# Turning new queries and keys for attention: 32x32 blocks on VectorE in place of 128x128 transposes on TensorE

## The chip, the cores and the metric

The kernel runs on one core of one Trainium2 chip. A core has five engines with a queue of instructions each, worked through in order: TensorE (PE in the profile; its weight loads are PEld), VectorE (DVE), ScalarE (ACT), GpSimd (POOL) and SyncE (SP). They share an on-chip memory of 128 partitions (SBUF); TensorE writes into accumulators (PSUM, eight banks of 128 partitions by 512 fp32). Transfers are issued by SyncE and GpSimd and carried out by 16 DMA engines. The metric is the device time of one execution in microseconds, the median of several runs.

## The reference

A tensor `x` of 32 batches, 32 positions and 512 features passes four residual stages, all in fp32. Each stage chooses weights by a token of the batch. The change concerns the fourth, attention over a paged cache with new queries, keys and values:

```
q = einsum('bsd,ed->bse', x, Wq)   # 32 heads of 128
k = einsum('bsd,ed->bse', x, Wk)   #  8 heads of 128
v = einsum('bsd,ed->bse', x, Wv)   #  8 heads of 128
q = rope(rmsnorm(q, q_norm_w), pos);  k = rope(rmsnorm(k, k_norm_w), pos)
k_all = concat([k_cache[block_table], k]);  v_all = concat([v_cache[block_table], v])
x = x + softmax(mask(q @ k_all.T * SCALE)) @ v_all @ Wo.T
```

`rmsnorm` divides each head of a row by the root of the mean of its squares and multiplies by a weight of 128 numbers. `rope` turns pairs of features (a feature of the first half of the head with its partner in the second) by an angle that grows with the position.

## The kernel before

The 1,024 rows of `x` (batch and position) make 8 row tiles of 128, four batches each. The program has three parts that follow each other.

**Residual stages 0 to 2.** A loop written out by hand sets TensorE's order. Eight row tiles pass through a pipeline with an offset of one tile from step to step: a mixing matmul (`mix`), transposes of `x` (`x1t`, `x2t`, `x3t`, each four 128x128 transposes on TensorE into PSUM and one copy on ScalarE, L383 and L384), a low-rank product, the base product and the adapter product (`adapt`, L439). After each product VectorE adds the result to `xs`. In the last steps of the same loop the projection of chunk 0 is done for each row tile.

**Projections.** The weights of queries, keys and values are 12 chunks `c` of 512 columns: 0 to 7 queries, 8 and 9 keys, 10 and 11 values, each four heads of 128. For every chunk and row tile (`project`, 96 in all, 80 with queries or keys), TensorE adds up four matmuls in a PSUM bank (L263; the trace shows two records for each fp32 matmul). Then, for queries and keys:

- ScalarE squares the bank (`sq`, L279), VectorE sums per head (`ss`, L281), ScalarE takes the root (`rms`, L283), VectorE its reciprocal (`rinv`, L285).
- VectorE multiplies the bank by the cosine table times the weight (`ra`, L287) and, in two halves, by the sine table (`rs`, L291 and L297). GpSimd adds the two (L303).
- VectorE multiplies the sum by `rinv`, spread over each head (L304).
- `store_heads`, called two tiles later (one tile later in chunk 0): TensorE turns the four heads (L312), ScalarE copies the four turned blocks out of PSUM into `st` (L314), in the order batch, head, position, and SyncE stores `st` to DRAM (L322), into `q_d` or `k_d`, which hold, for each batch, 128 features by heads and positions.

Value tiles are copied by ScalarE into one of two buffers `vs` (L273) and stored (L274). Outside the two loops marked as written out by hand, a scheduler orders each engine's instructions when the program is built, by the order of the source and by what is ready. Buffers: five PSUM banks for projections (`a_mm`), two for transposes (`a_tr`), one for the low-rank product (`a_lo`); three buffers each of `ra`, `st` and the small columns, two of `sq` and `rs`; two of a chunk's weights `wq` (L257).

SyncE's queue holds, in one order, the loads of weights, the stores of L322 and L274, and the loads for attention. Pages of batch 0 are loaded while chunks 0 to 2 are projected (L149, keys by SyncE, values by GpSimd). When the last key tile has been stored, the projection's buffers are given up (`turn.close()`), and batch 1's home takes their place: its new keys and queries are read back from `k_d` and `q_d` (L199, L200) and its 16 pages of keys and of values are loaded. The new values of the first batches are read from `v_d` (L229) once value tiles are stored.

**Attention.** 32 batches of 8 key heads, 256 units, in an order written out by hand for all engines: scores (L590, L591), mask and row maximum on VectorE (L597), exponentials on ScalarE (L604), division, four transposes (L621), products with values (L641), and the output projection after every four batches (L677). Batch b+1's data are loaded while batch b is worked on.

The core of the tail that the change rewrites:

```
for h in range(REP):
    nc.tensor.transpose(pt[:, h, :], a[:, h, :], ident)
st = tp.tile([P, BT, REP * S], F32, tag="st", name=f"st_{c}_{t}")
nc.scalar.copy(
    st.rearrange("d b (h s) -> d h b s", h=REP),
    pt.rearrange("d h (b s) -> d h b s", b=BT),
)
```

Of the kernel before, what the change touches and what calls it, by code (L numbers as in the profile page):

```python
# [11 lines left out]
F32 = mybir.dt.float32  # L12
I32 = mybir.dt.int32
AF = mybir.ActivationFunctionType
ALU = mybir.AluOpType
AX = mybir.AxisListType
PSUM = bass.MemoryType.PSUM
DRAM = bass.MemoryType.DRAM

P = 128  # L20
B, S, HID = 32, 32, 512
D, HQ, HK = 128, 32, 8
REP = HQ // HK
PAGES, PSIZE, NPP = 64, 32, 16
L = NPP * PSIZE
LT = L + S
NT = B * S // P
BT = P // S
# [25 lines left out]
def cond_resid_kernel(  # L54
# [18 lines left out]
    nc = tc.nc  # L73
# [3 lines left out]
    dram = ctx.enter_context(tc.tile_pool(name="scratch", bufs=1, space=DRAM))  # L77


    q_d = dram.tile([B, D, HQ * S], F32, name="q_d")  # L80
    k_d = dram.tile([B, D, HK * S], F32, name="k_d")
    v_d = dram.tile([B * S, HK * D], F32, name="v_d")


# [18 lines left out]
    ident = const.tile([P, P], F32, name="ident")  # L103
# [78 lines left out]
    homes, kts, vts, vns, news = {}, {}, {}, {}, {}  # L182
# [4 lines left out]
    def load_keys(b: int):  # L187
# [7 lines left out]
            mask, key_f, len_f[:, b : b + 1], -1.0e30, ALU.is_ge, ALU.mult  # L195
        )

    def load_new_keys(b: int):
        nc.sync.dma_start(out=kts[b][:, NPP, :], in_=k_d[b])  # L199
        nc.sync.dma_start(out=news[b][0], in_=q_d[b])  # L200

    def page_keys(b: int):
        return [kts[b][:, n, :] for n in range(NPP)]
# [30 lines left out]
    with ExitStack() as pa:  # L234
# [2 lines left out]
        turn = pa.enter_context(ExitStack())  # L237
        wp = turn.enter_context(tc.tile_pool(name="a_w", bufs=1))
        tp = turn.enter_context(tc.tile_pool(name="a_t", bufs=3))
        ps_mm = pa.enter_context(tc.tile_pool(name="a_mm", bufs=5, space=PSUM))  # L240
        ps_tr = pa.enter_context(tc.tile_pool(name="a_tr", bufs=2, space=PSUM))
        ps_lo = pa.enter_context(tc.tile_pool(name="a_lo", bufs=1, space=PSUM))


        x3t = xp.tile([P, KC, NT * P], F32, name="x3t")
# [9 lines left out]
        def load_qkv(c: int):  # L255
            ws[c] = wqp.tile([P, KC, HID], F32, tag="wq", name=f"wq_{c}")
            nc.sync.dma_start(out=ws[c], in_=w_qkv[c])  # L257

        def project(c: int, t: int):
            w = ws[c]  # L260
            ps = ps_mm.tile([P, HID], F32, tag="mm", name=f"qkv_{c}_{t}")
            for k in range(KC):
                nc.tensor.matmul(  # L263
                    ps,
                    x3t[:, k, t * P : (t + 1) * P],
                    w[:, k, :],
                    start=(k == 0),
                    stop=(k == KC - 1),
                )
            if c >= (HQ + HK) // REP:  # L270
                c0 = (c - (HQ + HK) // REP) * HID
                vs = xp.tile([P, HID], F32, tag="vs", name=f"vs_{c}_{t}", bufs=2)
                nc.scalar.copy(vs, ps)  # L273
                nc.sync.dma_start(out=v_d[t * P : (t + 1) * P, c0 : c0 + HID], in_=vs)  # L274
                return None
            i = 0 if c < HQ // REP else 1
            ps4 = ps.rearrange("p (h d) -> p h d", h=REP)
            sq = tp.tile([P, REP, D], F32, tag="sq", name=f"sq_{c}_{t}", bufs=2)
            nc.scalar.activation(sq, ps4, AF.Square)  # L279
            ss = tp.tile([P, REP], F32, tag="ss", name=f"ss_{c}_{t}")  # L280
            nc.vector.tensor_reduce(ss, sq, AX.X, ALU.add)  # L281
            rms = tp.tile([P, REP], F32, tag="rms", name=f"rms_{c}_{t}")
            nc.scalar.activation(rms, ss, AF.Sqrt, bias=eps_t, scale=1.0 / D)  # L283
            rinv = tp.tile([P, REP], F32, tag="rinv", name=f"rinv_{c}_{t}")
            nc.vector.reciprocal(rinv, rms)  # L285
            a = tp.tile([P, REP, D], F32, tag="ra", name=f"ra_{c}_{t}")
            nc.vector.tensor_tensor(  # L287
                a, ps4, cw[:, i, t, :].unsqueeze(1).to_broadcast([P, REP, D]), ALU.mult
            )
            s = tp.tile([P, REP, D], F32, tag="rs", name=f"rs_{c}_{t}", bufs=2)  # L290
            nc.vector.tensor_tensor(  # L291
                s[:, :, :H2],
                ps4[:, :, H2:],
                sw[:, i, t, :H2].unsqueeze(1).to_broadcast([P, REP, H2]),
                ALU.mult,
            )
            nc.vector.tensor_tensor(  # L297
                s[:, :, H2:],
                ps4[:, :, :H2],
                sw[:, i, t, H2:].unsqueeze(1).to_broadcast([P, REP, H2]),  # L300
                ALU.mult,
            )
            nc.gpsimd.tensor_tensor(a, a, s, ALU.add)  # L303
            nc.vector.tensor_tensor(  # L304
                a, a, rinv.unsqueeze(2).to_broadcast([P, REP, D]), ALU.mult
            )
            return c, t, a

        def store_heads(c: int, t: int, a):
            pt = ps_tr.tile([P, REP, P], F32, tag="tr", name=f"qt_ps_{c}_{t}")  # L310
            for h in range(REP):
                nc.tensor.transpose(pt[:, h, :], a[:, h, :], ident)  # L312
            st = tp.tile([P, BT, REP * S], F32, tag="st", name=f"st_{c}_{t}")
            nc.scalar.copy(  # L314
                st.rearrange("d b (h s) -> d h b s", h=REP),
                pt.rearrange("d h (b s) -> d h b s", b=BT),
            )
            if c < HQ // REP:
                dst, c0 = q_d, c * REP * S
            else:  # L320
                dst, c0 = k_d, (c - HQ // REP) * REP * S
            nc.sync.dma_start(  # L322
                out=dst[t * BT : (t + 1) * BT, :, c0 : c0 + REP * S].rearrange(
                    "b d x -> d b x"
                ),
                in_=st,
            )

        ready = []
# [1 line left out]
        def projected(c: int, t: int, lag: int):  # L331
            done = project(c, t)
            if done is not None:
                ready.append(done)
            if len(ready) > lag or (done is None and ready):
                store_heads(*ready.pop(0))

        with ExitStack() as p1:
# [169 lines left out]
            with tc.manual_schedule(engines={mybir.EngineType.PE}):  # L508
# [4 lines left out]
                for n in range(NT + 5):  # L513
# [24 lines left out]
                    if n == 4:  # L538
                        with tc.issue_after(picked_keys[-1]):
                            load_qkv(1)  # L540

        wop = ctx.enter_context(tc.tile_pool(name="b_wo", bufs=1, side="right"))
        wo = wop.tile([P, HQ, HID], F32, name="wo")
        vnp = ctx.enter_context(tc.tile_pool(name="b_vn", bufs=3, side="right"))
# [2 lines left out]
        for c in range(1, NCH):  # L547
            if c + 1 < NCH:
                load_qkv(c + 1)
            if c == 2:  # L550
                load_pages(0)
                load_values(0)
            if 3 <= c < 7:
                hs = slice((c - 3) * HQ // 4, (c - 2) * HQ // 4)
                nc.sync.dma_start(out=wo[:, hs, :], in_=w_o[:, hs, :])
            if c == (HQ + HK) // REP:

                while ready:
                    store_heads(*ready.pop(0))
                turn.close()  # L560
                load_new_keys(0)
                open_home(1)
                load_keys(1)
                load_new_keys(1)
                load_pages(1)
                load_values(1)
            for t in range(NT):
                projected(c, t, 2)
                if c == NCH - 1 and t == 2:
                    load_new_values(0)  # L570
                    load_new_values(1)
# [3 lines left out]
    tp = ctx.enter_context(tc.tile_pool(name="b_t", bufs=2))  # L575
# [119 lines left out]
    with tc.manual_schedule(engines=order):  # L695
        for n in range(N + 3):
            if n < N:
                b, g = units[n]
                if 1 <= b < B - 1:
                    at = B + (b + 1) * NPP  # L700
                    if g == 0:
                        load_keys(b + 1)
                        keys = Picked(nc.sync, k_cache, at, page_keys(b + 1), K_SHAPE)
                        load_new_values(b + 1)
                        load_new_keys(b + 1)
                        keys.transfer()
                    if g == 3:
                        values_in = Picked(nc.gpsimd, v_pages, at, page_values(b + 1), V_SHAPE)
                        values_in.transfer()
                scored.append(scores(b, g))  # L710
# [99 lines left out]
```

## Time and profile before

| what | value |
|---|---|
| median of 3 runs (lowest, highest) | 1353.11 us (1352.86, 1357.43) |
| the profiled execution | 1350.74 us |
| its span, from first to last instruction | 1348.8 us |
| TensorE busy | 1327.2 us (98%) |
| VectorE busy | 636.4 us (47%) |
| ScalarE busy | 536.8 us (40%) |
| GpSimd busy | 378.0 us (28%) |
| TensorE transposes of queries and keys (L312) | 320, 50.2 us busy |
| copies out of PSUM (L314) | 80, 46.2 us busy |
| divisions on VectorE (L304) | 80, 55.4 us busy |
| GpSimd's adds (L303) | 80, 101.0 us busy |
| first and last matmul of the projections | 56.8 and 489.8 us |

A row of a timeline gives the start in us, the duration, the engine, the line, the operation, output and inputs, shape and count; in brackets stands how long the engine was idle before it and what ended this wait. The duration of one instruction is longer than its step, the time from its start to the start of the next on the same engine, where neighbours overlap. Matmul ends are modelled, so TensorE's busy share says little of whether it has time to spare.

### The profile page before, as it was taken

What the parts mean: (1) busy time and instruction counts of PE and PEld (TensorE: products, weight loads), DVE (VectorE), ACT (ScalarE), POOL (GpSimd) and SP (SyncE); (2) the same over time, 40 slices, a digit from 0 to 9 for tenths busy, and PEclk for the clock granted to TensorE, in tenths of its full rate; (3) what the DMA queues carried; (4) which work ended last, traced back from release to release, by engine and by line L of the source; (5) the groups of instructions that cost most, each with busy time, mean ns of one, the idle gap of its engine ahead of it and who ended that gap; (6) DMA issues with size and microseconds to landing.
All of it is one profiled execution on the core that took longest, in us unless ns stands there. A gap on an engine that the chain in (4) does not pass through costs nothing.

```text
span 1348.8 us, 22925 instructions
## 1 busy us (share of the span) xinstructions
PE 1327.2 (98%) x6812; PEld 874.7 (65%) x6812; DVE 636.4 (47%) x1686; ACT 536.8 (40%) x1383; POOL 378.0 (28%) x618
## 2 busy tenths in 40 slices
PE   8999999999998989999999999999999999999998
PEld 4444444444444458858858867877876875885884
DVE  4333666666665016616625634633642651661650
ACT  1222333233232136616625634643642651661660
POOL 2302423323322202422422331340440431342220
PEclk9999999999999999999999999999999999999999
DMA  8977953333333717966985993892992993894740
GB/s 329 419 268 248 315 202 108 107 102 97 114 94 98 221 68 200 249 143 188 230 185 147 254 202 117 236 250 80 256 236 86 238 234 87 240 248 111 197 101 8
DMA packets 172667, 246.65 MB, mean 183 GB/s; under 512 B 22369, under 2 KB 141537, under 8 KB 166274
## 3 DMA queue, kind: packets, MB, share of 16 engines
q1 hardware_dynamic: 147714, 177.92, 44.8%
q0 software_dynamic: 24832, 67.27, 20.7%
q8 instruction: 57, 0.93, 0.3%
q14 instruction: 64, 0.52, 0.1%
HBM read 217.84 MB, written 27.26 MB: 182 GB/s over the span
## 4 chain that ended last, share of the span: by engine, by line
issue 48%; PE 13%; DVE 13%; POOLq 11%; POOL 10%; DMA 3%; ACT 0%; SPq 0%; ACTq 0%; DVEq 0%
POOLq L165 10%; POOL ra L303 6%; POOL vt L177 4%; DVE ra L304 3%; DVE ra L287 3%; DVE ss L281 3%; PE qkv L263 2%; PE adapt L439 2%; PE f_ps L677 2%; PE base L420 2%; DVE rs L297 2%; DVE rs L291 2%; POOLq L177 1%; PE o_ps L641 1%; DMA q_d<-st 1%
## 5 line engine op out<-in xcount | busy, mean ns | idle before, releaser
L177 POOL DMA_DIRECT2D vt<-in_v_cache_dram x480 | 241.4, 503 | 596.0 <-PE o_ps L641 424.1
L263 PE MATMUL qkv<-wq,x3t 128*128 128x512 f32 x768 | 345.1, 595 | 1.0 <-ACT vs L273 1.0
L623 ACT COPY pt<-p_ps 128x512 f32<-128x512 f32 x256 | 149.8, 585 | 419.6 <-PE p_ps L621 419.6
L597 DVE CUSTOM_DVE_ANT_0 pr<-s_ps,mask 128x544 f32<-128x544 f32 x256 | 185.5, 725 | 247.9 <-PE s_ps L591 196.1
L641 PE MATMUL o_ps<-pt,vt 128*128 128x128 f32 x2048 | 271.7, 275 | 1.4 <-DMA vt<-in_v_cache_dram 1.2
L641 PEld LDWEIGHTS o_ps<-pt,vt 128*128 128x128 f32 x2048 | 249.4, 192 | 3.2 <-issue 3.2
L263 PEld LDWEIGHTS qkv<-wq,x3t 128*128 128x128 f32 x768 | 140.0, 191 | 152.1 <-issue 150.2
L677 PE MATMUL f_ps<-wo,ot 128*128 128x512 f32 x512 | 221.5, 592 | 0.0
L604 ACT ACTIVATE pr<-pr,low 128x544 f32<-128x544 f32 x256 | 192.8, 753 | 0.8 <-DVE low L597 0.8
L303 POOL TENSOR_TENSOR ra<-ra,rs 128x512 f32<-128x512 f32 x80 | 101.0, 1262 | 277.0 <-DVE rs L297 275.4
L590 PE MATMUL s_ps<-kt,qt 128*128 128x288 f32 x512 | 174.2, 422 | 3.4 <-DVE low L597 2.7
L677 PEld LDWEIGHTS f_ps<-wo,ot 128*128 128x128 f32 x512 | 96.5, 190 | 117.8 <-issue 117.7
L591 PE MATMUL s_ps<-kt,qt 128*128 128x256 f32 x512 | 152.9, 380 | 1.7 <-issue 1.7
L621 PE MATMUL p_ps<-ident,pr 128*128 128x128 f32 x1024 | 154.1, 273 | 0.2 <-DVE pr L610 0.2
L621 PEld LDWEIGHTS p_ps<-ident,pr 128*128 128x128 f32 x1024 | 128.3, 141 | 26.1 <-issue 0.5
L610 DVE TENSOR_SCALAR pr<-pr,rden 128x512 f32<-128x512 f32 x256 | 124.6, 487 | 9.1
L591 PEld LDWEIGHTS s_ps<-kt,qt 128*128 128x128 f32 x512 | 97.4, 191 | 29.2 <-issue 2.4
L304 DVE TENSOR_TENSOR ra<-ra,rinv 128x512 f32<-128x512 f32 x80 | 55.4, 692 | 110.8 <-POOL ra L303 110.8
L681 DVE TENSOR_TENSOR xs<-xs,f_ps 128x512 f32<-128x512 f32 x8 | 5.5, 688 | 210.2 <-PE f_ps L677 210.2
L283 ACT ACTIVATE rms<-ss,eps_t 128x4 f32<-128x4 f32 x80 | 23.9, 298 | 186.1 <-DVE ss L281 185.9
L590 PEld LDWEIGHTS s_ps<-kt,qt 128*128 128x128 f32 x512 | 78.2, 192 | 16.4 <-DVE low L597 3.8
L614 ACT ACTIVATE pq<-pr,rden 128x32 f32<-128x32 f32 x256 | 79.6, 311 | 0.0
(90 smaller groups left out, 893.9 us busy)
## 6 DMA issues: line engine op xcount, KB each, us to landing
kt<-in_k_cache_dram SPq DMA_DIRECT2D x512, 128.0 KB, 5.4
vt<-in_v_cache_dram POOLq DMA_DIRECT2D x512, 128.0 KB, 5.5
wa<-in_w_adapt_dram SPq DMA_DIRECT2D x32, 1024.0 KB, 8.4
q_d<-st SPq DMA_DIRECT2D x64, 256.0 KB, 2.3
qt<-q_d SPq DMA_DIRECT2D x32, 512.0 KB, 6.0
wq<-in_w_qkv_dram SPq DMA_DIRECT2D x12, 1024.0 KB, 5.5
wo<-in_w_o_dram SPq DMA_DIRECT2D x4, 2048.0 KB, 15.5
k_d<-st SPq DMA_DIRECT2D x16, 256.0 KB, 2.3
```

Of the source, the lines that this page charges most:

```text
L165: nc.values_load(pk[0:1, n : n + 1], engines=(self.eng.engine,), min_val=0, max_val=self.src.shape[0] - 1, skip_runtime_bounds_check_becau ...
L177: self.eng.dma_start(out=out, in_=row)
L263: nc.tensor.matmul(ps, x3t[:, k, t * P : (t + 1) * P], w[:, k, :], start=(k == 0), stop=(k == KC - 1),)
L303: nc.gpsimd.tensor_tensor(a, a, s, ALU.add)
L590: nc.tensor.matmul(ps[:, first:L], q, kt4[:, :N_LOW, g, :], start=True, stop=True)
L591: nc.tensor.matmul(ps[:, L : first + LT], q, kt4[:, N_LOW:, g, :], start=True, stop=True)
L597: nc.vector.tensor_tensor_reduce(pr, ps[:, first : first + LT], mask, -SCALE, 3.0e38, ALU.add, ALU.min, low)
L604: nc.scalar.activation(pr, pr, AF.Exp, bias=low, scale=-1.0, accum_out=den)
L621: nc.tensor.transpose(pp[:, c, :], pr[:, c * P : (c + 1) * P], ident)
L623: nc.scalar.copy(pt, pp)
L641: nc.tensor.matmul(po[:, u, :P], vt[:, c, g * D : (g + 1) * D], pt[:, c, :], start=(c == 0), stop=False,)
L677: nc.tensor.matmul(pf, ot[:, h, :], wo[:, h, :], start=(h == 0), stop=(h == HQ - 1))
```

## The change

- `q_d` and `k_d` are laid out anew: row tile, row in the tile (128), block of 32 features (4), then heads and positions.
- In `project`, the division moves to ScalarE: four activations `Copy`, one for each head, 128x128, with the head's column of `rinv` as the scale.
- In `store_heads`, VectorE transposes every 32x32 block of the 128x512 tile in one instruction, from SBUF to SBUF. Inside a block, features and positions change places; the blocks stay with the 32 partitions of their batch. The transposes on TensorE and the copies on ScalarE are gone. `st` holds, in partition (batch, feature in the block), the block, head and position. It is stored as it is.
- `by_head_size` reads a batch's part back: 32 rows by 4 blocks, with blocks and rows exchanged, so that partition `k * 32 + d` receives feature `k * 32 + d`.
- The three PSUM pools are closed after the residual stages, and the projections of chunks 1 to 11 use one pool of eight banks (`a_all`).

```
-    q_d = dram.tile([B, D, HQ * S], F32, name="q_d")
-    k_d = dram.tile([B, D, HK * S], F32, name="k_d")
+    q_d = dram.tile([NT, P, D // S, HQ * S], F32, name="q_d")
+    k_d = dram.tile([NT, P, D // S, HK * S], F32, name="k_d")
...
+    def by_head_size(new: bass.AP, b: int):
+        t, j = divmod(b, BT)
+        return new[t, j * S : (j + 1) * S].rearrange("d k x -> k d x")
...
-        nc.sync.dma_start(out=kts[b][:, NPP, :], in_=k_d[b])
-        nc.sync.dma_start(out=news[b][0], in_=q_d[b])
+        nc.sync.dma_start(out=kts[b][:, NPP, :], in_=by_head_size(k_d, b))
+        nc.sync.dma_start(out=news[b][0], in_=by_head_size(q_d, b))
...
-            ps = ps_mm.tile([P, HID], F32, tag="mm", name=f"qkv_{c}_{t}")
+            ps = (ps_mm if c == 0 else ps_all).tile([P, HID], F32, tag="mm", name=f"qkv_{c}_{t}")
...
-            nc.vector.tensor_tensor(
-                a, a, rinv.unsqueeze(2).to_broadcast([P, REP, D]), ALU.mult
-            )
+            for h in range(REP):
+                nc.scalar.activation(a[:, h, :], a[:, h, :], AF.Copy, scale=rinv[:, h : h + 1])
...
-            pt = ps_tr.tile([P, REP, P], F32, tag="tr", name=f"qt_ps_{c}_{t}")
-            for h in range(REP):
-                nc.tensor.transpose(pt[:, h, :], a[:, h, :], ident)
-            st = tp.tile([P, BT, REP * S], F32, tag="st", name=f"st_{c}_{t}")
-            nc.scalar.copy(
-                st.rearrange("d b (h s) -> d h b s", h=REP),
-                pt.rearrange("d h (b s) -> d h b s", b=BT),
-            )
+            st = tp.tile([P, D // S, REP, S], F32, tag="st", name=f"st_{c}_{t}")
+            nc.vector.transpose(
+                st.rearrange("p k h s -> p h k s"), a.rearrange("p h (k d) -> p h k d", d=S)
+            )
...
             nc.sync.dma_start(
-                out=dst[t * BT : (t + 1) * BT, :, c0 : c0 + REP * S].rearrange(
-                    "b d x -> d b x"
-                ),
-                in_=st,
+                out=dst[t, :, :, c0 : c0 + REP * S], in_=st.rearrange("p k h s -> p k (h s)")
             )
...
+        banks.close()
+        ps_all = pa.enter_context(tc.tile_pool(name="a_all", bufs=8, space=PSUM))
```

More of the change, by code (lines that the diff above doesn't have):

```diff
@@ L239, in cond_resid_kernel @@
         tp = turn.enter_context(tc.tile_pool(name="a_t", bufs=3))
-        ps_mm = pa.enter_context(tc.tile_pool(name="a_mm", bufs=5, space=PSUM))
-        ps_tr = pa.enter_context(tc.tile_pool(name="a_tr", bufs=2, space=PSUM))
-        ps_lo = pa.enter_context(tc.tile_pool(name="a_lo", bufs=1, space=PSUM))
+        banks = pa.enter_context(ExitStack())
+        ps_mm = banks.enter_context(tc.tile_pool(name="a_mm", bufs=5, space=PSUM))
+        ps_tr = banks.enter_context(tc.tile_pool(name="a_tr", bufs=2, space=PSUM))
+        ps_lo = banks.enter_context(tc.tile_pool(name="a_lo", bufs=1, space=PSUM))
         x3t = xp.tile([P, KC, NT * P], F32, name="x3t")
```

## The prediction

> **What bounds the kernel now.** I read the stretches first, then the order of time inside one, then the chain of waits, then what releases the next stage. The profiled execution took 1350.74 us (span 1348.8); all sums below are made in its time.
>
> Busy time by stretch (us of the stretch, then busy us and instruction counts of TensorE, weight load, VectorE, ScalarE, GpSimd; granted clock; DMA share; GB/s):
>
> ```profile
> core 0: us, PE busy (x) PEld busy (x) DVE busy (x) ACT busy (x) POOL busy (x), PEclk, DMA share, GB/s
> 160.00:430.00 270.00, 268.06 (x799) 121.77 (x797) 173.83 (x400) 84.85 (x202) 83.94 (x67) 1.00 0.39 122
> 430.00:491.00 61.00, 57.86 (x136) 25.79 (x136) 3.90 (x8) 10.60 (x19) 9.74 (x18) 0.97 0.59 175
> 491.00:1349.00 858.00, 847.30 (x5184) 653.34 (x5184) 393.59 (x1126) 404.91 (x1090) 241.45 (x480) 1.00 0.71 178
> ```
>
> The change touches only work before 491 us; the 858 us of attention keep their instructions. From 160 to 430 TensorE looks full, but one period of VectorE shows otherwise:
>
> ```profile
> 249.52 0.68 DVE L287 TENSOR_TENSOR ra<-qkv,cw 128x512 f32<-128x512 f32 x1
> 250.12 0.17 DVE L285 RECIPROCAL rinv<-rms 128x4 f32<-128x4 f32 x1
> 250.20 0.39 DVE L291 TENSOR_TENSOR rs<-qkv,sw 128x256 f32<-128x256 f32 x1
> 250.51 0.41 DVE L297 TENSOR_TENSOR rs<-qkv,sw 128x256 f32<-128x256 f32 x1
> 252.36 0.69 DVE L304 TENSOR_TENSOR ra<-ra,rinv 128x512 f32<-128x512 f32 x1 [1.44 <-POOL ra L303]
> 252.97 0.68 DVE L281 TENSOR_REDUCE ss<-sq 128x4 f32<-128x512 f32 x1
> 253.57 0.68 DVE L287 TENSOR_TENSOR ra<-qkv,cw 128x512 f32<-128x512 f32 x1
> ```
>
> L287 comes round every 4.05 us. VectorE works in order: its division L304 waits 1.44 us for GpSimd's add, and nothing behind it can start. It idles nowhere else, so this ring sets the pace of some 70 tiles. TensorE has a little less to do:
>
> ```profile
> 249.62 3.60 PE L263 MATMUL qkv<-wq,x3t 128*128 128x512 f32 x8
> 253.20 0.63 PE L312 MATMUL qt_ps<-ident,ra 128*128 128x128 f32 x4
> 253.67 0.59 PE L263 MATMUL qkv<-wq,x3t 128*128 128x512 f32 x1
> ```
>
> Eight matmul records start 0.43 us apart (3.44 us a tile); four transposes add 0.43. Between 145.83 and 165.19, where TensorE has a backlog, its tiles do come every 3.87 us; later it follows VectorE at 4.05.
>
> After the last key tile SyncE's queue sets the time:
>
> ```profile
> 438.27 0.36 SPq L322 DMA_DIRECT2D k_d<-st  x1
> ...
> 442.20 13.19 SPq L149 DMA_DIRECT2D kt<-in_k_cache_dram  x16
> 455.49 15.50 SPq L274 DMA_DIRECT2D v_d<-vs  x8
> 472.71 1.30 SPq L229 DMA_DIRECT2D vn<-v_d  x2
> ...
> 481.85 2.46 SPq L229 DMA_DIRECT2D vn<-v_d  x4
> 484.41 6.96 SPq L274 DMA_DIRECT2D v_d<-vs  x5
> ```
>
> Batch 1's pages need room that opens only when the last key tile is stored; the value stores queue behind them, two `vs` buffers each wait for a store to land, and the first masked score (L597) waits 51.8 us for the last of these stores. TensorE's 15 remaining value tiles need 15 x 3.44 = 51.6 us, so both end together near 490. This matters: from the last key store to attention is some 52 us whatever TensorE gains.
>
> **The change, part by part.** In the changed program as built, VectorE and ScalarE take the tiles of chunks 1 to 9 mostly in pairs, an even tile e and an odd tile o. VectorE: ss, ra, rinv, rs, rs of e; ss, ra, rs, rs, rinv of o; transpose e, transpose o. ScalarE: square e, root e, square o, four scalings of e, root o, four scalings of o.
>
> *Removed:* 320 transposes on TensorE (0.43 us a tile), 80 PSUM copies on ScalarE (577 ns), 80 divisions on VectorE (692 ns).
>
> *Scalings, 320 of 128x128 with a column as factor.* Not in the trace. Nearest row: L614, 128x32 with such a factor, 311 ns. ScalarE's slope from its copies (270 ns at 128 elements, 580 at 512) is 0.80 ns an element, so 311 + 96 x 0.80 = 0.39 us. Neighbours overlap: the root L283 takes 0.30 and the next starts 0.20 after it; so 0.29 from start to start, and four take 3 x 0.29 + 0.39 = 1.26 us. Ends: 0.16 a step and 0.27 the last (L630, 128x128 copies), or 0.39 with no overlap. ScalarE has room: 85 of 270 us busy.
>
> *Block transpose, 80 of 128x512.* Not in the trace. VectorE's one-element rows L281, L287 and L304 take 0.68 to 0.69, with 0.60 from start to start; I take 0.60, since it also streams 512 elements a partition. Ends: 0.34 (the step of L463, 128x512, 0.42 long) and 1.26 (GpSimd's add of the same shape). [...]
>
> *The pair, from its first ss.* Handovers are as in the trace: L297 to GpSimd's add 0.56 from start to start, the add 1.29 with its handover, ss to root 0.72, root to rinv 0.33. VectorE starts: 0 ss, 0.60 ra, 1.20 rinv, 1.29 rs, 1.60 rs of e; 1.94 ss, 2.54 ra, 3.14 rs, 3.45 rs of o. Add of e is done at 1.60 + 0.56 + 1.29 = 3.45; scalings of e from there, root o at 3.45 + 4 x 0.29 = 4.61, rinv o at 4.94, transpose e 5.03 to 5.63. Add of o is done at 3.45 + 1.85 = 5.30, its scalings at 6.56, transpose o 6.59 to 7.19. The next square starts at 6.46 and is done at 7.09, hidden by the transpose. Period **7.19 us a pair, 3.60 a tile**, against 4.05. So the wait for GpSimd doesn't go; a pair pays it once, lengthened by the scalings (3.79 to 6.59, partly filled by transpose e). GpSimd's add of e now runs beside VectorE; that costs nothing in the trace where L422 (38.14, 0.69 us) or L281 (157.90) lie beside a GpSimd add.
>
> With the bounds: scalings at 0.16/0.27 put transpose o at 6.08 and the ring at 6.68, below TensorE's 6.88, so **3.44** a tile; scalings without overlap 7.73 a pair, **3.87**; transpose at 1.26 7.85, **3.93**; at 0.34 the square decides, 7.09.
>
> *Eight accumulators.* TensorE no longer waits for VectorE's finished tiles, only for a free bank, and may lead by eight tiles. Its total is not the bound above. At the switch of pools the first tile of chunk 1 waits until chunk 0's last tile is read.
>
> *Chunk 0, inside the residual stages.* These are TensorE's: four transposes (1.74 us) and a wait of 0.35 go before chunk 0's tile 5 (125.53 becomes 123.4). ScalarE and VectorE now hold their next copy or add behind the scalings, but the scalings of a tile squared at 91.41 would end near 96.7 (last rs 93.63, + 0.5, + 1.3, + 1.26), and the copy of x2t starts only at 97.46. Then chunk 0's tile 5 runs alone: 3.8 to its square, 0.6 to ss at 127.8, and 1.6 + 1.85 + 1.29 to its transpose, square of tile 6 in time for ss at 133.2; pair 6/7 to 140.4; chunk 1's first tile waits for its bank (137.1) and 3.8 of matmul, ss 141.5, alone again 5.4: the next ss at 146.9. Before it stood at 146.28: nothing is won until there.
>
> *Stores.* Same 256 KB in 512-byte pieces; one lands in 2.3 us, in up to 12.7 between 130 and 160 where the DMA share is 0.97. Three `st` buffers at 3.6 us allow 10.8, so VectorE now waits where ScalarE did: about 3 us in all, my choice between 0 and 6. Reading back is in rows of 4 KB and 1 KB as before: nothing.
>
> *Sum.* 71 tiles from 146.9: 146.9 + 71 x 3.595 + 3 = 405 for the last key store, against 438.3: **-33 us**. From there 52 us as before: one value store now stands ahead of the pages (-1); TensorE, done early, idles longer before attention, and after an idle 3.42 us at 428 eight records took 4.78 instead of 3.60 (clock 0.86 in that stretch): +1. So 1350.74 - 33 = 1317.7, and against the median of the runs, 1353.11 (2.4 above), 1320.
>
> **The rivals.**
> - *TensorE becomes the bound.* For: the cheap end of the scalings. 146.9 + 71 x 3.44 + 3 = 394, -44: 1309. Against: L614 says a factor column costs more than a plain copy.
> - *The ring stays longer,* by scalings without overlap (-13.6, 1340) or a transpose of 1.26 us (-9, 1344). Both together give 8.39 a pair, 4.20 a tile, +9: 1362.
> - *Slower: the block transpose streams 4-byte data at a quarter of the rate.* The place is VectorE's ring, where the transposes stand in order. Break-even is (438.3 - 3 - 146.9)/71 = 4.06 a tile, 8.12 a pair, a transpose of 1.53 us. At 4 x 0.60 = 2.4, transposes of e and o follow each other: 5.03 + 4.8 = 9.83 a pair, 4.92 a tile, +61: 1414. For: no row shows this operation. Against: no VectorE row of this shape is over 0.69 undisturbed.
> - *It doesn't shorten the stage:* if the stretch after the keys were held by a fixed DMA time, the 33 us would come back. Against: its first page load is released by the key store, so it moves along.
>
> **How the numbers follow.** Forecast (1312 to 1328) 0.58; TensorE bound (1304 to 1312) 0.15; longer ring but faster 0.12; no change, with both prices high, 0.06; slower 0.09. The likeliest is 1320. The range 1304 to 1344 takes in the single bounds and leaves out the last two and a little of the others. Differences under 0.5% can't be told from none here. Faster 0.85, same 0.06, slower 0.09.
>
> **What would show it.** Right: VectorE's transpose near 0.69 us; ss of even tiles 7.2 us apart; its largest wait at the transposes, for ScalarE; last key store near 405, attention from 458. Wrong: periods of 6.88 (TensorE), a transpose over 1.5 us, a wait for stores all along, or attention starting much less than 52 us after the last key store.

## The result, and the profile after

The changed kernel takes 1499.2 us (median of 4 runs, 1493.49 to 1506.45) against 1355.27 us for the kernel before (1352.86 to 1368.37, 4 runs): a ratio of 1.104, 95% interval 1.096 to 1.113 (ratios are estimated from the single runs, and are not exactly the quotient of the medians). The profiled execution took 1506.45 us, its span 1504.8.

Busy time by stretch of the changed kernel (columns as in the prediction). The first stretch is the projections, the second runs from the last key store to the first scores, the third is attention:

```profile
core 0: us, PE busy (x) PEld busy (x) DVE busy (x) ACT busy (x) POOL busy (x), PEclk, DMA share, GB/s
160.00:408.00 248.00, 248.00 (x580) 109.76 (x579) 177.40 (x406) 137.32 (x412) 86.35 (x68) 1.00 0.43 134
408.00:467.00 59.00, 35.53 (x80) 15.33 (x79) 0.60 (x2) 8.46 (x15) 7.88 (x16) 0.84 0.60 163
467.00:1505.00 1038.00, 901.25 (x5184) 689.45 (x5184) 393.58 (x1126) 405.08 (x1089) 242.34 (x480) 0.92 0.60 147
```

The projections end 30 us earlier, as was meant. Attention issues the same 5184 matmuls, and takes 1038 us instead of 858. TensorE is busy for 901 of them, before 847: 137 us idle instead of 11, and 54 us more busy at a mean granted clock of 0.92 instead of 1.00. 126 + 54 is the whole loss of 180.

What TensorE waits for, from 430 us on (us in total, times, longest):

```profile
PE s_ps L593 <- DMA kt<-in_k_cache_dram: 58.3, 7, 11.6
PE s_ps L594 <- DMA vn<-v_d: 30.7, 6, 7.8
PE s_ps L594 <- DMA kt<-in_k_cache_dram: 23.1, 11, 6.5
...
PE o_ps L644 <- DMA vt<-in_v_cache_dram: 13.7, 4, 5.5
```

These four make 125.8 us, about the idle time just found (the lines left out hold two waits at the end of the projections, 23.4 us, and six short ones). But the loads that they name, pages and new values, are not those that the change touched. The chain of waits names the one that it did touch (the two lines of the page, shares of the span):

```profile
PE 53%; DMA 30%; SPq 3%; DVE 2%; issue 1%; ACT 1%; POOL 1%; POOLq 0%; DVEq 0%; ACTq 0%
PE qkv L270 15%; PE f_ps L680 15%; DMA qt<-q_d 14%; DMA kt<-in_k_cache_dram 13%; PE o_ps L644 8%; PE s_ps L594 5%; PE s_ps L593 5%; PE p_ps L624 4%; DMA vn<-v_d 1%; SPq L235 1%; PE o_ps L655 1%; DMA v_d<-vs 1%; SPq L166 1%; SPq L178 1%; DVE ss L288 1%
```

The link between both is SyncE's queue. Its own waits between 500 and 1300 us, in the changed kernel:

```profile
SPq L178 <- DMA qt<-q_d: 155.5, 26, 11.9
SPq L685 <- DVE xs L684: 91.3, 6, 20.6
SPq L178 <- DMA kt<-in_k_cache_dram: 64.5, 80, 1.9
```

and in the kernel before:

```profile
SPq L682 <- DVE xs L681: 169.7, 7, 25.2
SPq L199 <- PE s_ps L591: 61.8, 28, 18.8
SPq L177 <- DMA kt<-in_k_cache_dram: 16.3, 25, 1.2
SPq L177 <- DMA qt<-q_d: 7.1, 8, 1.4
```

Before, the queue stood little at the page loads (L177, 23.4 us in these lines); what it waited for was room, given free by the scores (L199), and finished rows to store (L682). After, the page loads (L178) stand behind the load of the new queries for 155.5 us, 26 times, nearly once a batch. In order of time, at one such place of the changed kernel (start, duration, what; from the chain of waits):

```profile
668.90 18.64 DMA qt<-q_d
...
687.56 9.99 DMA kt<-in_k_cache_dram
...
697.56 3.95 DMA kt<-in_k_cache_dram
...
701.76 1.19 PE s_ps L594 x2
```

The queries are issued at 668.90 and hold the chain for 18.64 us, one of the longer such places, and only then do the pages get through. TensorE still works off the batch at hand, with a stop of 5.35 us for a value page before 684.40; then it waits for the pages of keys, 3.41 us before 699.43 and 1.60 before 701.76. The 16 page loads behind it took the queue 27.94 us; at the same place before, 14.13:

```profile
668.90 0.85 SPq L206 DMA_DIRECT2D qt<-q_d  x1
669.96 27.94 SPq L178 DMA_DIRECT2D kt<-in_k_cache_dram  x16
```

```profile
674.71 1.24 SPq L200 DMA_DIRECT2D qt<-q_d  x1
676.14 14.13 SPq L177 DMA_DIRECT2D kt<-in_k_cache_dram  x16
```

(the changed kernel first, the kernel before second; SPq is SyncE's queue, x the number of issues).

### The profile page after: what moved, and what is told of

Its sections match the earlier page's. It is cut to its first block, busy times and chain, and to the rows that moved or that the text cites. A ratio compares the mean times of both kernels' runs of the same rounds, so it can differ in the third digit from the quotient of the medians.

```text
span 1504.8 us, 22628 instructions
## 1 busy us (share of the span) xinstructions
PE 1336.8 (89%) x6492; PEld 885.4 (59%) x6492; DVE 636.4 (42%) x1686; ACT 595.6 (40%) x1623; POOL 379.4 (25%) x618
## 2 busy tenths in 40 slices
DMA packets 171901, 246.63 MB, mean 164 GB/s; under 512 B 21602, under 2 KB 140770, under 8 KB 165507
## 4 chain that ended last, share of the span: by engine, by line
PE 53%; DMA 30%; SPq 3%; DVE 2%; issue 1%; ACT 1%; POOL 1%; POOLq 0%; DVEq 0%; ACTq 0%
PE qkv L270 15%; PE f_ps L680 15%; DMA qt<-q_d 14%; DMA kt<-in_k_cache_dram 13%; PE o_ps L644 8%; PE s_ps L594 5%; PE s_ps L593 5%; PE p_ps L624 4%; DMA vn<-v_d 1%; SPq L235 1%; PE o_ps L655 1%; DMA v_d<-vs 1%; SPq L166 1%; SPq L178 1%; DVE ss L288 1%
## 5 line engine op out<-in xcount | busy, mean ns | idle before, releaser
L178 POOL DMA_DIRECT2D vt<-in_v_cache_dram x480 | 242.3, 505 | 762.3 <-PE o_ps L644 564.7
L270 PE MATMUL qkv<-wq,x3t 128*128 128x512 f32 x768 | 335.1, 598 | 17.0 <-ACT vs L280 14.1
L644 PE MATMUL o_ps<-pt,vt 128*128 128x128 f32 x2048 | 285.6, 284 | 13.7 <-DMA vt<-in_v_cache_dram 13.7
L644 PEld LDWEIGHTS o_ps<-pt,vt 128*128 128x128 f32 x2048 | 263.5, 201 | 15.5 <-DMA vt<-in_v_cache_dram 11.2
L593 PE MATMUL s_ps<-kt,qt 128*128 128x288 f32 x512 | 187.0, 449 | 73.3 <-DMA kt<-in_k_cache_dram 58.3
L594 PE MATMUL s_ps<-kt,qt 128*128 128x256 f32 x512 | 169.1, 415 | 54.2 <-DMA vn<-v_d 30.7
L624 PE MATMUL p_ps<-ident,pr 128*128 128x128 f32 x1024 | 164.4, 286 | 0.2 <-DVE pr L613 0.2
L594 PEld LDWEIGHTS s_ps<-kt,qt 128*128 128x128 f32 x512 | 103.9, 207 | 92.3 <-DMA kt<-in_k_cache_dram 19.0
L624 PEld LDWEIGHTS p_ps<-ident,pr 128*128 128x128 f32 x1024 | 138.2, 150 | 31.3 <-issue 5.9
L312 ACT ACTIVATE ra<-ra,rinv 128x128 f32<-128x128 f32 x320 | 102.2, 390 | 98.9 <-POOL ra L310 98.9
L593 PEld LDWEIGHTS s_ps<-kt,qt 128*128 128x128 f32 x512 | 83.5, 204 | 88.4 <-issue 65.8
L319 DVE STREAM_TRANSPOSE st<-ra 128x512 f32<-128x512 f32 x80 | 56.4, 705 | 52.5 <-ACT ra L312 40.2
```

The source lines that it names most:

```text
L178: self.eng.dma_start(out=out, in_=row)
L270: nc.tensor.matmul(ps, x3t[:, k, t * P : (t + 1) * P], w[:, k, :], start=(k == 0), stop=(k == KC - 1),)
L312: nc.scalar.activation(a[:, h, :], a[:, h, :], AF.Copy, scale=rinv[:, h : h + 1])
L593: nc.tensor.matmul(ps[:, first:L], q, kt4[:, :N_LOW, g, :], start=True, stop=True)
L594: nc.tensor.matmul(ps[:, L : first + LT], q, kt4[:, N_LOW:, g, :], start=True, stop=True)
L624: nc.tensor.transpose(pp[:, c, :], pr[:, c * P : (c + 1) * P], ident)
```

## The experiments

**Theory A.** The new read has an outermost dimension of four steps (the four blocks of 32 features) where the old one had 128 rows. The supposition: such a load runs on few of the DMA engines, takes long, and holds up the page loads behind it in SyncE's queue. **Rival B,** supposed as well: the rows that it reads lie 16 KB apart, and this order in DRAM is slow. **Rival C:** it takes SyncE longer to issue it (552 ns against 432), and the queue has no room for that. Beside e1 to e4 the kernel before took 1363.2 us.

| kernel | us (runs) | ratio to before, 95% interval | last key store issued (end) | first scores | attention |
|---|---|---|---|---|---|
| before | 1355.27 (4) | 1 | 438.6 | 491.1 | 857.7 |
| changed | 1499.2 (4) | 1.104 (1.096 to 1.113) | 408.7 | 466.8 | 1038.0 |
| e1, four loads each | 1386.28 (4) | 1.012 (1.002 to 1.022) | 408.9 | 458.9 | 927.7 |
| e2, two loads each | 1696.69 (1) | | 412.5 | 473.6 | 1221.4 |
| e3, padded rows | 1503.16 (1) | | 412.5 | 470.2 | 1031.3 |
| e4, four stores | 1327.6 (4) | 0.976 (0.969 to 0.984) | 412.3 | 466.0 | 859.9 |
| e6, before, four steps | 1550.22 (1) | | 441.1 | 517.1 | 1031.2 |
| e8, division on VectorE | 1366.28 (10) | 1.002 (0.999 to 1.006) | 444.6 | 495.9 | 864.0 |
| e9, pages later | 1329.14 (6) | 0.978 (0.973 to 0.982) | 412.1 | 461.0 | 861.0 |
| e10, five accumulators | 1349.57 (4) | 0.989 (0.984 to 0.995) | 423.6 | 484.6 | 867.2 |
| e11, four value buffers, pages last | 1315.76 (6) | 0.968 (0.965 to 0.972) | 412.8 | 447.3 | 862.1 |
| e12, four value buffers | 1323.77 (4) | 0.975 (0.971 to 0.979) | 412.0 | 455.9 | 859.2 |
| e13, e4 with reads cut | 1405.81 (1) | | 413.0 | 465.0 | 939.2 |
| e14, before with e11's edits | 1355.21 (10) | 0.998 (0.994 to 1.002) | 440.3 | 491.5 | 857.0 |

The last three columns come from the profiled execution, attention being the span's end less the first scores. Ratios are to the kernel before, run on the same chip beside it; its median was 1355 to 1363 us. e2, e3, e6 and e13 ran once; runs of one kernel differ by up to 27 us, and the losses read from e2, e6 and e13 are 79 us and more.

**e1, the read cut in four.** The changed kernel, with one load of 32 rows for each block:

```
t, j = divmod(b, BT)
for k in range(D // S):
    r = slice(k * S, (k + 1) * S)
    nc.sync.dma_start(out=kts[b][r, NPP, :], in_=k_d[t, j * S : (j + 1) * S, k])
    nc.sync.dma_start(out=news[b][0][r], in_=q_d[t, j * S : (j + 1) * S, k])
```

> The changed kernel with each read-back of new keys and queries cut into four loads, one for each block of 32 features (32 rows into 32 partitions); the same bytes from the same addresses, six more issues a batch. Theory A (a load whose outermost dimension has four steps runs on only a few DMA engines, which hold up the page loads behind it): attention, from the first score to the end, falls from 1038 us back to 858 to 875, the projections stay (last key store near 408), and the time is 1315 to 1335. Theory B (the rows, 16 KB apart in DRAM, are slow to read): nothing changes, near 1500. Theory C (the longer issue of these two loads, 0.55 to 0.61 us in place of 0.32 to 0.43, delays SyncE's queue): with eight issues in place of two it gets no faster than 1500.

1386.28 us. Attention falls from 1038 to 928, 110 of the 180 us. The theory's direction holds, but not its number; what keeps the other 70 is left to e13.

**e2, the read cut in two,** with two steps in the outermost dimension of each load:

```
for k in (0, 2):
    r = slice(k * S, (k + 2) * S)
    nc.sync.dma_start(out=kts[b][r, NPP, :], in_=by_head_size(k_d, b)[k : k + 2])
    nc.sync.dma_start(out=news[b][0][r], in_=by_head_size(q_d, b)[k : k + 2])
```

> The changed kernel with each read-back cut into two loads of two blocks each, so that the outermost dimension has two steps. Theory A: fewer engines still carry the 640 KB of a batch; slower than the changed kernel, by my estimate from its 32.4 us a batch about 36 us a batch, 1560 to 1650. Theory B (row distance) and theory C (issue): within 2% of the changed kernel's 1499.

1696.69 us. Four small loads repaired most of it, two make it much worse: attention 1221 us. The loss in attention is 364 us, against 180 with four steps: half as many steps, twice the loss. Both kernels move the same bytes in the same 171901 packets, so packet size is not it. The forecast of 1560 to 1650 had the direction and was too low. The queue's own waits from 500 to 1600 us:

```profile
SPq L178 <- DMA qt<-q_d: 265.8, 49, 11.0
...
SPq L178 <- DMA kt<-k_d: 31.5, 25, 3.9
```

The page loads now stand behind the keys' load too.

**e3, padding.** The changed kernel with 256 bytes behind each row in DRAM, so that the rows of a block no longer lie at a multiple of 16 KB:

```
-    q_d = dram.tile([NT, P, D // S, HQ * S], F32, name="q_d")
-    k_d = dram.tile([NT, P, D // S, HK * S], F32, name="k_d")
+    q_d = dram.tile([NT, P, D // S, HQ * S + 64], F32, name="q_d")
+    k_d = dram.tile([NT, P, D // S, HK * S + 64], F32, name="k_d")
```

> The changed kernel with 256 bytes of padding behind each row of the two DRAM tensors, so that rows lie 4352 bytes (queries) and 1280 bytes (keys) apart, blocks' rows four times that. One load each, as in the changed kernel. Theory A: no change, 1480 to 1520. Theory B (rows a power of two apart collide): back to 1315 to 1340.

1503.16 us: no difference from the changed kernel. That the rows lie a multiple of 16 KB apart is not the cause; rows that lie next to each other come in e6. (The two reads leave the padding out, with `[:, :, : HK * S]` and `[:, :, : HQ * S]`.)

**e4, the blocks put in place by the store instead.** DRAM and the read are those of before; the store is cut in four, one for each batch, with 32 rows each:

```
for j in range(BT):
    nc.sync.dma_start(
        out=dst[t * BT + j, :, c0 : c0 + REP * S].rearrange("(k d) x -> d k x", d=S),
        in_=st[j * S : (j + 1) * S].rearrange("p k h s -> p k (h s)"),
    )
```

> The changed kernel with the old layout of the two DRAM tensors (batch, feature, head and position): the blocks are put in place by the store, cut into four, one for each batch (32 partitions), and the read-back is the old single load of 128 rows. Theory A: attention back to 858 to 865 us; 240 more store issues of about 0.36 us in the projections, 1.4 us of SyncE's queue a tile of 3.6, should hide; 1315 to 1335. Theory B: the same, since the reads have the old addresses. If the stores' issue is not hidden, the last key store comes later than 408.

1327.6 us, faster than both kernels. Attention is back at 860 us, and the projections keep their gain: with 320 stores instead of 80 the last key store comes about 4 us later. Of the queue's wait (500 to 1300 us) little is left:

```profile
SPq L178 <- DMA qt<-q_d: 9.8, 13, 1.5
```

**e6, the same read in the kernel before.** So far the four-step read only occurred beside the rest of the change. Here the kernel before gets a gap behind every 32 rows, which leaves four steps outermost (its store is cut in four for that); TensorE still transposes and VectorE divides:

```
+    q_d = dram.tile([B, D // S, S + 1, HQ * S], F32, name="q_d")
+    k_d = dram.tile([B, D // S, S + 1, HK * S], F32, name="k_d")
...
+        nc.sync.dma_start(out=kts[b][:, NPP, :], in_=k_d[b, :, :S, :])
+        nc.sync.dma_start(out=news[b][0], in_=q_d[b, :, :S, :])
```

> The kernel before, with one thing of the change: a batch's keys and queries lie in DRAM as four blocks of 32 rows with a gap behind each block, so that the read's outermost dimension has four steps instead of 128. The rows stay next to each other inside a block, TensorE still transposes, VectorE still divides. The store is cut in four, one for each block. Theory A (a read whose outermost dimension has four steps is carried by few DMA engines, and holds up the page loads behind it): attention about 1035 to 1080 us instead of 858, in all 1530 to 1580. Rival D (the loss in attention needs the changed kernel's DRAM order, rows of one block 16 KB apart, or its projection part): attention 858, in all 1350 to 1362.

1550.22 us, attention 1031: the loss of the changed kernel, without the changed kernel. Inside a block the rows lie next to each other here, so B falls altogether. The stretch ahead of attention is longer too, 76 us instead of 52.5. The queue's wait from 500 to 1300 us is the same:

```profile
SPq L177 <- DMA qt<-q_d: 145.0, 24, 11.3
```

**The packets of these reads.** The trace keeps the start, time and size of every DMA packet. The queries of a batch come in 128 packets of 4 KB, the only ones of this size on SyncE's queue. Over 30 batches, from the start of a batch's first such packet to the end of its last, and how many are in flight:

| kernel | steps outermost | us (median) | in flight, mean (median of the batches) | in flight, most |
|---|---|---|---|---|
| before | 128 | 3.3 | 8.5 | 15 to 21 |
| e4 | 128 | 3.3 | 8.5 | 16 to 21 |
| changed | 4 | 9.0 | 3.4 | 5 to 7 |
| e6 | 4 | 8.9 | 3.6 | 6 or 7 |
| e2 (two loads, one of the keys between them) | 2 | 21.5 | 1.3 | 3 or 4 |

A packet takes 0.21 to 0.25 us on the mean in all five. So fewer of them run side by side (3.4 and 1.3 instead of 8.5), and with 3.6 in e6 this does not depend on the rest of the change. A packet's record doesn't name its engine: that few engines carry the load fits these counts, and stays the author's supposition.

**e13, what e1 still lost.** e4 with each read cut in four loads of 32 rows, at DRAM addresses as before:

```
for k in range(D // S):
    r = slice(k * S, (k + 1) * S)
    nc.sync.dma_start(out=kts[b][r, NPP, :], in_=k_d[b, r])
for k in range(D // S):
    r = slice(k * S, (k + 1) * S)
    nc.sync.dma_start(out=news[b][0][r], in_=q_d[b, r])
```

> The kernel with four stores a tile and the rows of a batch next to each other in DRAM (1327.6), with the two reads of a batch cut into eight loads of 32 rows. Each load's outermost dimension has 32 steps, and the DRAM order is that of before. It tells what the four-load version of the changed kernel (1386) still lost in attention, 928 instead of 858 us. Theory Q (six more issues in SyncE's queue, which has no room in a batch): attention 910 to 940, in all 1380 to 1405. Rival (the DRAM order of the changed kernel, rows of a block 16 KB apart): attention 858 to 865, in all 1325 to 1335.

1405.81 us, attention 939: it loses 79 us, in e1's neighbourhood (70), with the DRAM order of before. So e1's rest does not come from its DRAM order. The issues of one batch in e13:

```profile
618.70 2.73 SPq L239 DMA_DIRECT2D vn<-v_d  x4
621.54 1.92 SPq L207 DMA_DIRECT2D kt<-k_d  x4
624.98 2.71 SPq L210 DMA_DIRECT2D qt<-q_d  x4
627.89 12.01 SPq L178 DMA_DIRECT2D kt<-in_k_cache_dram  x16
```

Eight issues take 1.92 + 2.71 us, where the two of before took 0.34 + 1.24 at the place shown above; another batch of e13 has 1.74 + 1.81. Over 30 batches of the trace the issues of these reads take 100 us in e13 and 24 in e4: the 76 us more are about the 79. The smaller loads themselves are no slower: from issue to landing those of the queries take 2.8 us (median) and e4's single one 6.0, those of the keys 4.3 and 4.1. Rival C, then, was not empty: by these sums an issue in this queue costs attention nearly its full length. It does not explain the changed kernel, though: there the two issues take 0.62 and 0.55 us instead of 0.34 and 0.43, which makes 12 us in 31 batches, not 180.

**e8, the division back on VectorE.** e4, with one `tensor_tensor` multiplication per tile (L311) in place of the four activations:

> The kernel with four stores a tile and the read of before (1327.6), with the division by the rms put back on VectorE as one 128x512 multiplication a tile; transposes stay on VectorE and the eight accumulators stay. Theory R (the wait for GpSimd's add is what costs, and it can be filled): in the order as built most divisions have a block transpose or a sum ahead of them, inside the wait, so a tile takes 0.60 + 0.31 + 0.56 + 1.29 + 0.60 = 3.36 where all else fits in the wait and up to 4.2 where it doesn't: last key store 395 to 430, in all 1312 to 1345, the same as with the division on ScalarE within 1.3%. Rival (the division's place on ScalarE is what won the time): the ring of before, 4.05, plus a transpose of 0.60 in it, 4.65 a tile: last key store 146.9 + 71 x 4.65 = 477, in all about 1392.

1366.28 us: both forecasts miss. One tile of VectorE in e8:

```profile
299.99 0.69 DVE L311 TENSOR_TENSOR ra<-ra,rinv 128x512 f32<-128x512 f32 x1 [0.79 <-POOL ra L310]
300.60 0.70 DVE L320 STREAM_TRANSPOSE st<-ra 128x512 f32<-128x512 f32 x1
301.23 0.14 DVE L292 RECIPROCAL rinv<-rms 128x4 f32<-128x4 f32 x1
301.41 0.69 DVE L294 TENSOR_TENSOR ra<-qkv,cw 128x512 f32<-128x512 f32 x1
302.02 0.41 DVE L298 TENSOR_TENSOR rs<-qkv,sw 128x256 f32<-128x256 f32 x1
302.35 0.41 DVE L304 TENSOR_TENSOR rs<-qkv,sw 128x256 f32<-128x256 f32 x1
302.68 0.67 DVE L288 TENSOR_REDUCE ss<-sq 128x4 f32<-128x512 f32 x1
304.15 0.69 DVE L311 TENSOR_TENSOR ra<-ra,rinv 128x512 f32<-128x512 f32 x1 [0.79 <-POOL ra L310]
```

The division comes round every 4.16 us, before every 4.05. The sum `ss` has moved into the wait for GpSimd, which shrinks from 1.44 to 0.79 us; the transpose stands behind the division, outside the wait, and takes that back. In the order as built, then, the transposes alone win nothing in VectorE's ring; here the division has to leave it as well.

**e10, five accumulators.** e4 with `bufs=5` in the pool of the projections:

> The kernel with four stores a tile and the read of before (1327.6), with five accumulators for the projections instead of eight. Theory (VectorE's ring sets the pace, TensorE's lead is worth nothing): last key store within 4 us of 412, in all 1323 to 1333. Rival (the lead of eight tiles covers the transposes' lag): 3.6 us of wait for a bank every few tiles, last key store 425 to 440, in all 1340 to 1355.

1349.57 us: the theory, that TensorE's lead is worth nothing, fails, and the rival's sum holds. The last key store comes 11 us later than in e4, just short of the rival's 425. The two profiled executions differ by 26 us; of the other 15 half lie in the stretch ahead of attention, where TensorE waits 21.8 us for a value buffer instead of 14.6, and half in attention, unexplained. TensorE's waits between 130 us and the last key store, first in e10, then in e4:

```profile
PE qkv L270 <- DVE rs L304: 15.1, 5, 4.8
```

```profile
PE qkv L270 <- DMA wq<-in_w_qkv_dram: 3.3, 2, 2.6
PE qkv L270 <- DVE rs L304: 2.8, 1, 2.8
```

The last reader of a bank is the second `rs` (L304): TensorE waits 15.1 us for a free bank with five, 2.8 with eight. In e4 and e10 the scheduler's order on VectorE is not as even as the changed kernel's pairs; that this unevenness is what a lead of eight tiles covers is a reading, and was not tried by itself.

**e9, e12 and e11, the stretch ahead of attention.** In e4 it still takes 54 us. The queue of SyncE in that stretch of e4:

```profile
415.07 17.37 SPq L150 DMA_DIRECT2D kt<-in_k_cache_dram  x16
432.79 16.62 SPq L281 DMA_DIRECT2D v_d<-vs  x10
```

Value stores stand behind batch 1's pages, and TensorE idles 14.6 us for ScalarE, which waits for one of two value buffers. e9 takes `load_pages(1)` and `load_values(1)` to the middle of the last value chunk:

> The kernel with four stores a tile and the read of before (1327.6), with batch 1's page loads issued during the last value chunk instead of ahead of the first one, so that the value stores no longer stand behind 16 page loads in SyncE's queue. Theory (the stretch from the last key store to attention, 54 us, is held by SyncE's queue: value stores behind page loads, TensorE 14.6 us idle for the value buffers and some 9 us before the first score): the stretch shrinks to about 33 us, attention unchanged at 858 to 862, in all 1303 to 1312. Rival (batch 1's pages then come too late for its scores, and the time reappears as waits of its first scores): 1322 to 1332.

1329.14 us, no gain over e4: the theory's 1303 to 1312 fails, but not by the rival's mechanism: the first scores come at 461.0, and TensorE still waits 15.3 us for ScalarE, ScalarE 46.2 us in 13 pieces for value stores to land. e12 leaves the loads where they are and takes four value buffers (`vs`, `bufs=4`):

> The kernel with four stores a tile and the read of before (1327.6), with four value buffers instead of two and nothing else. Theory (as for its neighbour): part of TensorE's 14.6 us of idle time goes, but the value stores still stand behind 16 page loads in SyncE's queue: stretch 40 to 50 us instead of 54, in all 1314 to 1325. Rival (the queue alone holds the stretch): 1325 to 1331.

1323.77 us, within its forecast, and a ratio of 0.975 beside e4's 0.976: no difference that the runs can tell. First scores at 455.9, 44 us behind the last key store. e11 does both, with the page loads behind all value chunks:

> The kernel with four stores a tile and the read of before (1327.6), with four buffers for value tiles on their way to DRAM instead of two, and batch 1's page loads issued behind the value stores. In the run that only moved the page loads, ScalarE still waited 46 us in 13 pieces for the two value buffers, since the moved loads ran beside the stores, and TensorE 15.3 us for ScalarE. Theory (the stores' time to land, times too few buffers, holds the stretch between the last key store and attention): the stretch shrinks from 49 to 54 us to 33 to 40, attention stays at 858 to 862, in all 1303 to 1315. Rival (the late page loads of batch 1 then hold up its first scores, by what the stretch gave): 1322 to 1332.

1315.76 us, the fastest version, first scores at 447.3. It was only slightly above its forecast of 1303 to 1315. SyncE's queue in e11:

```profile
415.07 18.78 SPq L281 DMA_DIRECT2D v_d<-vs  x12
433.94 5.19 SPq L235 DMA_DIRECT2D vn<-v_d  x8
```

The value stores stand behind no page load any more. e14 makes the same two edits in the kernel before:

> The kernel before, with the two edits of the fastest version so far (four value buffers, batch 1's page loads behind the value stores) and nothing of the change. Theory: before, TensorE needs 15 x 3.44 = 51.6 us for the value tiles behind the last key store, so the queue's 52 us lie beside TensorE's own work, and the edits are worth little without the faster projections: last key store 438, first scores 486 to 491, in all 1346 to 1354. Rival (the edits gain by themselves): first scores below 480, in all below 1342.

1355.21 us, a ratio of 0.998 (0.994 to 1.002), first scores at 491.5. There TensorE itself needs the time behind the last key store, as the prediction said ("both end together near 490"), and the edits are worth nothing until the projections are faster.

## Why the prediction was wrong

**The step that failed** is "Reading back is in rows of 4 KB and 1 KB as before: nothing." The rows were indeed the same, and the queries of a batch come in 128 packets of 4 KB in both kernels. What the step left out is the outermost dimension of the access pattern: four steps. The runs price it: 180 us in attention with four steps (173 alone, in the kernel before, e6), 364 with two (e2), about 2 with 128 (e4). From four steps to two the loss doubles, and the packets go the same way: 8.5 in flight on the mean with 128 steps, 3.4 with four, 1.3 with two. Why they do is not shown: no run counts the engines of a load.

**The queue of before would have warned.** The prediction saw attention as untouched, since its instructions stay. But its rounds read what the change lays down, and the lines of before shown above have the load of the queries at 674.71 and 16 page loads right behind it, 14.13 us long: what holds up the one holds up the others (155.5 us of the queue's waits in the changed kernel). That the queue has little room shows only in e13, where 2.5 us more of issues a batch come out as 2.6 us more of attention.

**The granted clock** was costed in one stretch only. In attention it falls to 0.92 on the mean beside TensorE's waits, and the same matmuls are busy 54 us longer, of the 180.

**What was right** is the projection part. Of the changed kernel, rows of VectorE and ScalarE over one pair:

```profile
305.92 0.64 DVE L288 TENSOR_REDUCE ss<-sq 128x4 f32<-128x512 f32 x1
...
309.36 1.28 ACT L312 ACTIVATE ra<-ra,rinv 128x128 f32<-128x128 f32 x4 [1.98 <-POOL ra L310]
...
310.96 0.70 DVE L319 STREAM_TRANSPOSE st<-ra 128x512 f32<-128x512 f32 x1
311.21 1.28 ACT L312 ACTIVATE ra<-ra,rinv 128x128 f32<-128x128 f32 x4 [0.38 <-POOL ra L310]
312.39 0.57 ACT L286 ACTIVATE sq<-qkv 128x512 f32<-128x512 f32 x1
312.58 0.71 DVE L319 STREAM_TRANSPOSE st<-ra 128x512 f32<-128x512 f32 x1 [0.92 <-ACT ra L312]
313.21 0.64 DVE L288 TENSOR_REDUCE ss<-sq 128x4 f32<-128x512 f32 x1
```

- The pair takes 313.21 - 305.92 = 7.29 us, forecast 7.19. Four scalings take 1.28, forecast 1.26. The transpose takes 0.705 on the mean of 80, forecast near 0.69. The transpose waits for ScalarE, as forecast (40.2 us over the 80).
- The last key store is issued at 408.2, forecast 405, before 438.3. The pairs begin 2 us late, with `ss` at 149.05 (forecast 146.9), and are 0.1 us longer; VectorE's waits for stores, put at 3 us, make 1.9.
- "From there 52 us as before" was 6 too low: 58.6 to the first scores. The page loads of batch 1 stand behind a four-step read here too; with the read of before this stretch takes 54 us (e4), and there as here TensorE waits 14 us for a value buffer.
- The sum: 1317.7, and 3 for the last key store, 6 for the stretch behind it, 180 for attention, make 1506.7; measured 1506.45.
- "Eight accumulators" had no term of their own. In e4's form five instead of eight give a ratio of 0.989 instead of 0.976, with the last key store 11 us later (e10).
- **The slower rival** had its place on VectorE, with a transpose of 2.4 us, four times the step of a multiplication. No run shows that factor; the transpose measured 0.705 us. The side that the time went to was given 0.09, for a mechanism that did not occur; the read that the change rewrote had no rival at all.

**Left open:** why SyncE's queue stands still behind a slow load rather than issuing on; that wait is inferred from semaphores, and no run shows what happens in it. And what VectorE's transposes, the division and the accumulators are worth one by one: that is known only from taking the last two back, one at a time: of e4's gain of 2.4% five accumulators instead of eight give up 1.3 points (e10, under half of it ahead of the last key store), the division 2.6 (e8).

## What to carry to other kernels

When a change rewrites a transfer's access pattern, count the steps of its outermost dimension, not only the bytes of a row: here, on the DRAM side of the read, four in place of 128 cost 180 us, more than five times what the rest of the change won. Put the awkward order on the side that has time: the same blocks placed by the stores, in e4, cost 2 us in attention and 4 ahead of it. And ask what stands behind a transfer in its queue: the view of the queue's own waits named the slow load (155.5 us), where TensorE's waits named its neighbours (125.8 us).

## What the runs showed of the hardware

- A block transpose of 128x512 fp32 on VectorE takes 705 ns (mean of 80), about as long as a multiplication of that shape (0.68 to 0.69).
- A load of 512 KB with four steps outermost has 3.4 packets in flight on the mean and takes 9.0 us for them (median), with 128 steps 8.5 packets and 3.3 us. At the place shown it held the chain for 18.64 us.
- In attention, six more issues a batch of some 0.42 us each in SyncE's queue (76 us over 30 batches, e13) came with 79 us more.
- With idle gaps of TensorE of up to 11.6 us in attention, 137 us in all, the mean granted clock there is 0.92 instead of 1.00 (four steps), with 300 us in all 0.86 (two steps). The loss there is more than the idle time: 180 us lost for 126 more idle, and 364 for 289.
